# Two-layer cross-attention with image tokens on one core: a written beginning, loads queued behind the stacks, a scaling on ScalarE, and fixed PSUM banks

## The chip, the core and the metric

The kernel runs on one core of a Trainium2 chip. The engines have these names in the profile: PE is TensorE (matrix products; PEld is its weight load), DVE is VectorE, ACT is ScalarE, POOL is GpSimd, SP is SyncE, which issues most DMAs. The metric is the device time of one execution in microseconds (us). Times below are medians of executions without the profiler; every row of a profile comes from one profiled execution of its own.

## The reference

Two cross-attention layers run one after the other. `x` is 16 sequences of 256 queries with 320 channels (20 heads of 16), `ctx` is 16 contexts of 256 tokens with 512 channels. A context is cut into text tokens and image tokens.

```python
# layer 0: text = ctx[:, :77], ip = ctx[:, 77:]
q, k_text, v_text = x @ Wq, text @ Wk, text @ Wv
text_out = softmax(q_h @ k_h.T * scale) @ v_h                    # per head
scores = q_h @ ip_k_h.T * scale                                  # per head
text_probs = softmax(q @ k_text.T * scale)                       # over all channels at once
sem = (text_probs @ text) @ ip.T * scale                         # "semantic" scores
ip_probs = softmax(scores + 0.5 * sem[:, None]) * mask[:, None]  # mask: one number per query
out = (text_out + ip_probs @ ip_v_h) @ Wout + bout + x
# layer 1: text = ctx[:, :-4], ip = ctx[:, -4:]; sem is a cosine, per head, of probs_t @ text with ip;
# otherwise the same form
```

All of it is float32.

## The kernel before, in words

**Numbers in two halves.** A float32 matrix is cut into a rounded high half and a low half (`halves`: a cast on ACT, line 150, and a subtraction on DVE or POOL, line 153). A product is then three products, high x high, high x low and low x high (`prod`, line 238; `prod_m`, line 248, for the queries' and keys' columns, which come in three column blocks m = 0, 1, 2 of 128, 128 and 64 channels). `split` (lines 583 to 585) does the same for the queries' input x (tile `xq`, halves `hq`).

**Slots.** The main loop has 80 slots for layer 0 and 80 for layer 1: slot k is image k // 5 and head group k % 5 (4 heads of 20). A slot of layer 0 consists of

- `score0` for slot k+2, in two halves t = 0, 1 of the queries: four products (line 728) into the tile S, which is two banks of PSUM, and two reduces to maxima on DVE (lines 729, 730);
- `maxima0` for slot k+1: the maxima are turned (line 736, an X tile), copied to `mt`, and written by four small DMAs into the query stack `qs` (line 740); these DMAs are issued by ACT;
- `turned0` for slot k: scores again, keys on partitions (line 752, two T tiles), the exponential on ACT (line 755) into the tiles P in SBUF, and a multiplication by the semantic factor `rs` on POOL (line 758);
- `attend0` for slot k-1: 12 products with the values (line 785) into the PSUM tile P, then `settle0` (lines 796 to 805): a transpose and a normalization on DVE, of which `tmp` (line 802) is the last to read that bank;
- `stacks0` for slot k+4: the slot's keys, queries and semantic rows are brought into the stacks `ks` and `qs` by DMAs of SP. Keys (`kd`) and queries (`qd`) come out of DRAM, where the kernel wrote them after computing them.

**Side work.** What the images need besides is done in pieces between the parts of a slot. A list of tasks gives each piece a due time in slots (`task`, `fill`, `shifted`; `RAMP` compresses times around slot 0): `keys0` (the keys of a pair of images; it starts with the load of a pair's contexts, `context`, tiles `rawc`, halves `cta` and `ctb`), `queries0` (the load of x, `split`, `project` on lines 595 and 598, and a write `qd`), `tokens0` (token products, tile M), `values0_` (values into `vr`, line 401 for the copy), `semantic0` and `close0` (output projection, bias, residual). `semantic0` makes the semantic factor of an image: scores q @ k_text for both halves t (line 651) in an X tile each, copied and summed into `sp` (lines 653, 654), a softmax over the 77 text tokens (maximum, exponential on ACT with its sum, then a reciprocal on line 665 and a multiplication on line 666, both on DVE), a transpose (line 670) whose halves are `tph`, and a product with the tokens.

**Order.** Before the main loop `begin()` runs, in which the order of all engines is the written one: loads of the first contexts and weights (`all_halves`), first keys (`keys_first`), first queries, values and stacks, up to the first slots. In the main loop only PE keeps the written order; SP, ACT, DVE and POOL are ordered by a planner, which issues a load as early as its buffer allows. `queued` ties an instruction behind the last instruction that `anchor` marked on the same engine, without a wait.

**PSUM.** One pool holds 8 banks. A T tile (2 buffers), a P tile (1) or an X tile (3; all side work and the maxima) takes whichever of banks 2 to 7 is free at that point of the plan; the two-bank tile S has banks 0 and 1.

Of the kernel before, what the change touches and what calls it, by code (L numbers as in the profile page):

```python
# [17 lines left out]
S = 256  # L18
# [31 lines left out]
def xattn2(  # L50
# [31 lines left out]
    def dma(out, in_):  # L82
        nc.sync.dma_start(*(f(ap) if ap.dtype == FR else ap for ap in (out, in_)))  # L83
# [43 lines left out]
    nc.scalar.copy(ident_r, ident)  # L127
    tmask = const_tile([128, 7], "tmask")
    dma(tmask, tmask_d)
# [46 lines left out]
    def in_turn(parts, wait, tag="raw", eng=nc.vector):  # L176

        ahead, parts, tags = [], list(parts), tag.split()
        for i in range(len(parts) + 1):
# [6 lines left out]
            for j in new:  # L186
# [4 lines left out]
                dma(raw, src)  # L191
# [27 lines left out]

    def all_halves(jobs, rings):  # L220

        waiting = []
        for src, hi, lo, tag in jobs:
            while sum(w[3] == tag for w in waiting) == rings[tag]:
                halves(*waiting.pop(0)[:3])
            raw = buf(tag, [128, 512], bufs=rings[tag])
            raw = raw[:, : src.shape[1]] if len(src.shape) == 2 else raw.rearrange("p (k n) -> p k n", k=src.shape[1])
            dma(raw, src)
            waiting.append((hi, lo, raw, tag))
        for w in waiting:  # L230
            halves(*w[:3])
# [30 lines left out]
    def context(b, n, wait=0):  # L262
# [8 lines left out]
        yield from in_turn(parts, wait, "rawc raw" if b == 2 and n == 2 else "rawc", nc.gpsimd if wait and b != 2 else nc.vector)  # L271
        if n == 2:
# [3 lines left out]

    ct = [buf(t, [128, 2, 512], FR, bufs=2, name="ct") for t in ("cta", "cta", "ctb", "ctb")]
    ctx0 = [(cT_d[k * 128 : (k + 1) * 128, : 2 * S], ct[k][:, 0], ct[k][:, 1]) for k in range(4)]
# [6 lines left out]
    RINGS = {"P": SIZES["NP"], "raw": SIZES["RAW"], "rawc": 2}  # L285
    all_halves(
        [job for k in range(4) for job in (
            (*ctx0[k], ("rawc", "raw")[k // 2]), (rows(wk0_d, k), *rounded(wkt[:, k]), "P"))],
        RINGS,
    )  # L290
    x0 = buf("xq", [128, 3, S])
    dma(x0, xT_d[0].rearrange("(k p) t -> p k t", p=128))
    all_halves(
# [28 lines left out]
    for v in vr:  # L322
        nc.gpsimd.memset(v, 0.0)
        for t in range(2):
            nc.vector.tensor_scalar_add(
                vcols(v, V0W)[:, t, :, 16], vcols(v, V0W)[:, t, :, 16], tmask[:, t : t + 1]
            )
# [967 lines left out]
```

## Time and profile before

| | before |
|---|---|
| median of 3 runs | 1550.69 us (1549.12 to 1552.69) |
| the profiled execution's own time | 1542.26 us |
| its span | 1540.4 us |
| granted clock of TensorE, mean | 0.978 |
| PE busy | 1441.0 us (94%) |
| DVE busy | 1207.8 us (78%) |
| POOL busy | 1203.6 us (78%) |
| PEld busy | 1162.6 us (75%) |
| ACT busy | 872.8 us (57%) |

The span runs from the first to the last instruction of the profiled execution; its own time has 1.86 us more for what lies around it, and the median of the runs without profiler is 8.43 us above that. Rows of the timeline give start, length, engine and line, operation, tiles written and read, and how many instructions are merged into the row; a bracket at the end gives the idle time before it and what ended it. Rows of waits give who waited, for whom, and then total us, number of waits and the longest. A granted clock of 1.00 is TensorE's full rate.

### The profile page before, as it was taken

The numbers are of one execution on the slowest core, as the hardware profiler recorded it, in microseconds if no ns is written. First come the engines' busy times: TensorE is split into PE (matmuls) and PEld (weight loads), VectorE is DVE, ScalarE is ACT, GpSimd is POOL, SyncE is SP. The second block draws the span as 40 slices with busy tenths as digits, with TensorE's granted clock in tenths as the row PEclk, the third lists the DMA queues.
The fourth block names the chain that finished last, engine by engine and source line by source line (L and its number), as shares of the span: only waits on it lengthen the run. The fifth ranks groups of instructions, "written<-read, shape, count | busy, mean of one in ns | idle before, by whom it ended". The sixth has DMA issues, their size and how long they took to land.

```text
span 1540.4 us, 36105 instructions
## 1 busy us (share of the span) xinstructions
PE 1441.0 (94%) x12726; PEld 1162.6 (75%) x12726; DVE 1207.8 (78%) x2659; ACT 872.8 (57%) x1941; POOL 1203.6 (78%) x1274
## 2 busy tenths in 40 slices
PE   6789999999999989788999999999999999999996
PEld 5678888878787878567777777777777777777764
DVE  6458888777777788867778888888887887788885
ACT  5345555555564545546665666566656666666561
POOL 4258797979797978878587788877987798779785
PEclk9889999999999999989999999999999999999997
DMA  6756777676766666765444344444444344434311
GB/s 208 204 179 175 218 192 215 189 218 188 217 192 201 190 202 172 207 199 153 117 123 117 115 137 110 117 130 120 117 119 136 108 121 124 132 106 113 100 32 36
DMA packets 228815, 233.04 MB, mean 151 GB/s; under 512 B 38410, under 2 KB 198508, under 8 KB 228620
## 3 DMA queue, kind: packets, MB, share of 16 engines
q1 hardware_dynamic: 226428, 229.44, 52.5%
q8 instruction: 102, 1.67, 0.5%
q10 hardware_dynamic: 2208, 1.30, 0.3%
q14 instruction: 77, 0.63, 0.1%
HBM read 118.04 MB, written 77.10 MB: 127 GB/s over the span
## 4 chain that ended last, share of the span: by engine, by line
PE 57%; POOL 12%; DVE 11%; DMA 7%; issue 4%; ACT 3%; SPq 2%; ACTq 1%; DVEq 0%; POOLq 0%
PE X L238 12%; PE X L923 11%; POOL wt L914 5%; PE P L785 5%; PE X L595 5%; PE S L728 4%; PE P L935 3%; PE T L752 3%; PE P L945 3%; PE T L875 2%; PE S L881 2%; POOL P L758 2%; DMA qs<-qd 2%; SPq L83 2%; DVE wt L924 2%
## 5 line engine op out<-in xcount | busy, mean ns | idle before, releaser
L758 POOL TENSOR_TENSOR P<-P,rs 128x512 f32<-128x512 f32 x320 | 413.9, 1316 | 121.0 <-ACT P L755 120.5
L914 POOL TENSOR_TENSOR wt<-P,ctb 128x512 f32<-128x512 f32 x320 | 410.4, 1306 | 86.8 <-ACT ctb L913 85.8
L923 PE MATMUL X<-ctb,gm 128*128 128x512 f32 x1120 | 305.9, 402 | 6.4 <-DVE wt L924 6.3
L755 ACT ACTIVATE P<-T 128x512 f32<-128x512 f32 x320 | 176.3, 594 | 172.7 <-PE T L752 104.4
L924 DVE TENSOR_TENSOR wt<-X,wt 128x512 f32<-128x512 f32 x320 | 216.6, 681 | 46.9 <-PE X L923 41.2
L923 PEld LDWEIGHTS X<-ctb,gm 128*128 128x128 f32 x1120 | 195.7, 189 | 39.8 <-DVE wt L924 9.2
L895 ACT ACTIVATE P<-T 128x512 f32<-128x512 f32 x320 | 173.3, 594 | 76.5 <-PE T L875 74.2
L913 ACT ACTIVATE ctb<-P 128x512 fp32r<-128x512 f32 x320 | 187.0, 627 | 44.1 <-PE X L923 33.1
L883 DVE TENSOR_REDUCE mn<-S 128x4 fp32r<-128x1008 f32 x160 | 191.2, 1195 | 0.0
L730 DVE TENSOR_REDUCE mn<-S 128x4 fp32r<-128x716 f32 x160 | 142.3, 889 | 0.0
L785 PE MATMUL P<-P,vr 128*32 128x256 f32 x1920 | 127.7, 397 | 3.6 <-DVE mx L665 1.2
L728 PE MATMUL S<-ks,qs 125*128 125x256 f32 x640 | 117.5, 307 | 7.5 <-DMA qs<-tph 4.1
L728 PEld LDWEIGHTS S<-ks,qs 125*128 125x128 f32 x640 | 89.0, 196 | 43.1 <-issue 36.2
L752 PE MATMUL T<-qs,ks 127*128 127x256 f32 x640 | 108.4, 290 | 11.9 <-DVE tmp L802 6.4
L1011 POOL TENSOR_TENSOR r<-u,rs 128x40 f32<-128x40 f32 (+2 forms) x17 | 108.7, 6395 | 3.9 <-DVE u L1008 3.8
L752 PEld LDWEIGHTS T<-qs,ks 127*128 127x128 f32 x640 | 90.9, 194 | 14.9 <-DVE tmp L802 6.9
L729 DVE TENSOR_REDUCE mn<-S 128x4 fp32r<-128x308 f32 x160 | 74.2, 464 | 32.4 <-PE S L728 31.6
L796 DVE STREAM_TRANSPOSE nt<-P 128x512 f32<-128x512 f32 x80 | 56.9, 711 | 48.6 <-PE P L785 48.1
L785 PEld LDWEIGHTS P<-P,vr 128*32 128x32 f32 x1920 | 57.4, 112 | 45.6 <-issue 7.0
L595 PE MATMUL X<-hq,wE 128*128 128x256 f32 x512 | 79.2, 294 | 10.6 <-ACT hq L583 5.0
L935 PE MATMUL P<-P,v1t 128*32 128x256 f32 x1280 | 86.4, 388 | 0.2 <-DVE wt L924 0.2
L945 PE MATMUL P<-wt,zone 128*32 128x256 f32 x1280 | 85.1, 379 | 0.3 <-DVE wt L924 0.3
(235 smaller groups left out, 3004.9 us busy)
## 6 DMA issues: line engine op xcount, KB each, us to landing
qd<-q SPq DMA_DIRECT2D x96, 256.0 KB
qs<-tph SPq DMA_DIRECT2D x64, 308.0 KB
rawc<-in_cT_dram SPq DMA_DIRECT2D x60, 256.0 KB
qs<-qd SPq DMA_DIRECT2D x80, 192.0 KB
ks<-kd SPq DMA_DIRECT2D x80, 192.0 KB
ks<-kd SPq DMA_DIRECT2D x160, 96.0 KB
qs<-qd SPq DMA_DIRECT2D x160, 96.0 KB
kd<-kst SPq DMA_DIRECT2D x57, 256.0 KB
```

The lines of the kernel that those rows point to most:

```text
L238: last = mm(out, lhs(a, k), rhs(b, k), start=i == 0, stop=i == len(terms) - 1)
L728: mm(sp[:, h], Q[: XROW + T0, h, t * 128 : (t + 1) * 128], K[: XROW + T0, h], start=True, stop=True)
L752: mm(st[p][:, j], K[:KS0, 2 * p + j, t * 128 : (t + 1) * 128], Q[:KS0, 2 * p + j], start=True, stop=True)
L755: exp = anchor(nc.scalar.activation(pt, st[p], AF.Exp, scale=SCALE))
L758: anchor(nc.gpsimd.tensor_mul(pt, pt, rs[:, t : t + 1].to_broadcast([128, 2, S])))
L785: mm(pv[32 * s : 32 * s + 32, o : o + S], v[:, vt, h : h + 32], P[k, s // 2][:, t, s % 2], start=vt < 2, stop=vt != 1,)
L883: anchor(nc.vector.tensor_reduce(maxes[k + 2][:, t], sp[:, :, :T1], axis=AX.X, op=ALU.max))
L895: anchor(nc.scalar.activation(P[k, u][:, t], st[u], AF.Exp, scale=SCALE))
L913: nc.scalar.activation(R[k, u][:, t], P[k, u][:, t], AF.Copy, scale=0.5)
L914: anchor(nc.gpsimd.tensor_sub(W[k, u][:, t], P[k, u][:, t], f(R[k, u][:, t])))
L923: mm(yp, gm[:, gb], R[k, u][:, kt], start=i == 0, stop=i == len(blocks[n]) - 1)
L924: nc.vector.tensor_mul(W[k, u][:, n], yp, W[k, u][:, n])
```

## The change

Four edits:

- `begin()` is written anew. The loads of the first contexts and weights are issued in an order written there (`first`, `land`, `cast`), `keys_first` makes the text keys of all three column blocks context tile by context tile, the query weights come ahead of the image-token weights, the first stack is issued ahead of the second image's query writes, and the second image's values come later. `constants`, `marks` and `fields` hold what was memsets and small loads: the memset of `qs` and most of that of `vr` go. `turns` gives some X tiles of the beginning a bank of T or P.
- In `context` the loads of both images of a pair (from the third pair on), and in `queries0` those of x for the odd images from image 3 on (`late`), are `queued` behind the key stack's DMA, which is now an anchor on SP. The due time of the odd x load goes from -4.4 to -5.4.
- In `semantic0` the multiplication on line 666 becomes a copy with a scale on ACT.
- In PSUM layer 0 (the profile's first layer) gets fixed tiles: S has its two banks (`whole`), T two of its own and P one (`kept`, taken in turn by `own`); X tiles have the other three. Layer 1 takes its tiles from the pool as before. (The code names the layers 0 and 1.)

```diff
...
+    turns = []
+
     def bank(tag="X"):
-        return ps.tile([128, 512], F32, tag=tag, name=tag, bufs=BANKS[tag])
-
-    def scores():
-
-        return ps.tile([128, 1024], F32, tag="S", name="S", bufs=1).rearrange("p (h t) -> p h t", h=4)
+        turn = turns.pop(0) if turns and tag == "X" else "X"
+        return own(turn) if turn != "X" else ps.tile([128, 512], F32, tag=tag, name=tag, bufs=BANKS[tag])
+
+    whole = ps.tile([128, 1024], F32, tag="S0", name="S", bufs=1)
+    kept = {t: [0] + [ps.tile([128, 512], F32, tag=f"{t}{i}", name=t, bufs=1) for i in range(BANKS[t])] for t in "TP"}
+
+    def own(tag):
+
+        n, *ring = kept[tag]
+        kept[tag][0] += 1
+        return ring[n % len(ring)]
+
+    def scores(kept=False):
+
+        s = whole if kept else ps.tile([128, 1024], F32, tag="S", name="S", bufs=1)
+        return s.rearrange("p (h t) -> p h t", h=4)
...
-                dma(raw, src)
+                (queued if later else lambda inst: inst)(dma(raw, src))
...
-        yield from in_turn(parts, wait, "rawc raw" if b == 2 and n == 2 else "rawc", nc.gpsimd if wait and b != 2 else nc.vector)
+        yield from in_turn(parts, wait, "rawc raw" if b == 2 and n == 2 else "rawc", nc.gpsimd if wait and b != 2 else nc.vector, n == 2 and b > 2)
...
+    def constants():
+
+        nc.vector.memset(zone, 0.0)
+        nc.vector.memset(zone[:, 21:22], 1.0)
+        for i in range(SIZES["NR"]):
+            nc.gpsimd.memset(f(ks[i]), 0.0)
+        nc.gpsimd.memset(f(buf("q", [128, 2, 3, S], FR))[64:, :, 2], 0.0)
+        for v in vr:
+            nc.gpsimd.memset(v[:, :, H * V0W :], 0.0)
+            nc.gpsimd.memset(vcols(v, V0W)[:, 2, :, 16], 1.0)
+
+    def marks():
+
+        for v in vr:
+            for t in range(2):
+                nc.gpsimd.tensor_copy(vcols(v, V0W)[:, t, :, 16], tmask[:, t : t + 1].to_broadcast([128, H]))
+
+    def fields():
+
+        ind0 = buf("nt", [128, 2, 8, 32], bufs=2, name="ind0").rearrange("p a f c -> p (a f c)")[:2, :S]
+        dma(ind0, ind0_d)
+        ind0r = buf("mt", [8, S], FR, name="ind0r")[:2]
+        nc.scalar.copy(ind0r, ind0)
+        for i in range(SIZES["NR"]):
+            dma(ks[i][XROW + T0 : KS0], ind0r.unsqueeze(1).to_broadcast([2, 4, S]))
...
-        for w, lo, hi, a, z in ((wk0, 0, T0 + 1, 0, T0), (wki0, T0 - 1, S, T0, S)):
+        out = lambda lo, hi: bank()[:, : 2 * (hi - lo)].rearrange("p (b t) -> p b t", b=2)
+        kp = [out(0, T0 + 1) for m in range(3)]
+        for k in range(4):
             for m in range(3):
-                kp = bank()[:, : 2 * (hi - lo)].rearrange("p (b t) -> p b t", b=2)
-                prod_m(kp, w, m, lambda s, k: ct(s, k)[:, :, lo:hi], 4)
-                n = 64 if m == 2 else 128
-                evacuate(kst[m][:, 0, :, a:z], kst[m][:, 1, :, a:z], kp[:, :, a - lo : z - lo], m)
-                if a:
-                    keys_out(kd[0][0], m, kst[m], slice(0, 1))
-                else:
-                    nc.gpsimd.tensor_copy(kt[:n, m, :, :, :T0], f(kst[m][:n, :, :, :T0]))
-                yield
+                terms = ((0, 0), (0, 1), (1, 0))[: 3 if m < 2 else 2]
+                for i, (a, c) in enumerate(terms):
+                    mm(kp[m], wk0(a, k, m), ct(c, k)[:, :, : T0 + 1], start=k + i == 0, stop=k == 3 and i == len(terms) - 1)
+            yield
+        for m in range(3):
+            n = 64 if m == 2 else 128
+            evacuate(kst[m][:, 0, :, :T0], kst[m][:, 1, :, :T0], kp[m][:, :, :T0], m)
+            nc.gpsimd.tensor_copy(kt[:n, m, :, :, :T0], f(kst[m][:n, :, :, :T0]))
+        yield
+        for m in range(3):
+            kp = out(T0 - 1, S)
+            prod_m(kp, wki0, m, lambda s, k: ct(s, k)[:, :, T0 - 1 : S], 4)
+            evacuate(kst[m][:, 0, :, T0:], kst[m][:, 1, :, T0:], kp[:, :, 1:], m)
+            keys_out(kd[0][0], m, kst[m], slice(0, 1))
+            yield
...
-    def load(src, tag):
+    def load(src, tag, late=False):
         x = buf(tag, [128, 3, S])
-        dma(x, src.rearrange("(k p) t -> p k t", p=128))
+        order = queued if late else lambda inst: inst
+        order(dma(x, src.rearrange("(k p) t -> p k t", p=128)))
         return x
 
     def queries0(b):
-        x = x0 if b == 0 else load(xT_d[b], "xq")
-        yield
-        xs = split(x, tmask[:, 5:6], nc.gpsimd if b else nc.vector, "hq")
+        x = b and load(xT_d[b], "xq", b > 1 and b % 2)
+        yield
+        xs = split(x, tmask[:, 5:6], nc.gpsimd, "hq") if b else xs0.pop()
         yield
         return (yield from queries(0, xs))
...
             nc.vector.reciprocal(zs, zs)
-            nc.vector.tensor_scalar_mul(tp, tp, zs)
+            nc.scalar.activation(tp, tp, AF.Copy, scale=zs)
...
-                dma(K[0:XROW], stack_rows(kd[0][b // 2][:, :, b % 2], g))
+                anchor(dma(K[0:XROW], stack_rows(kd[0][b // 2][:, :, b % 2], g)))
...
-        sp = scores()
+        sp = scores(True)
...
-        st = [bank("T").rearrange("p (h t) -> p h t", h=2) for p in range(2)]
+        st = [own("T").rearrange("p (h t) -> p h t", h=2) for p in range(2)]
...
-        v, pv = get("v0", b), bank("P")
+        v, pv = get("v0", b), own("P")
...
-        task(("q0", 2 * c + 1), shifted(n, -4.4, -4, -3, -2.8, -2), lambda b=2 * c + 1: queries0(b))
+        task(("q0", 2 * c + 1), shifted(n, -5.4, -4, -3, -2.8, -2), lambda b=2 * c + 1: queries0(b))
...
     def begin():
         parts = lambda *keys: [step(key) for key in keys if key in tasks]
-        k0, q0, s0, m0, q1 = ("k0", 0), ("q0", 0), ("s0", 0), ("m0t", 0), ("q0", 1)
-        parts(k0, k0, k0, q0, q0, q1, q0, q0, q0)
+        k0, q0, s0, m0, m1, q1, v0, v1 = ("k0", 0), ("q0", 0), ("s0", 0), ("m0t", 0), ("m0t", 1), ("q0", 1), ("v0", 0), ("v0", 1)
+        landed = {}
+
+        def land(*names):
+            for n in names:
+                src, hi, lo, tag = first[n]
+                raw = landed[n] = buf(tag, [128, 512], bufs=SIZES["NP"] if tag == "P" else 2)[:, : src.shape[1]]
+                dma(raw, src)
+
+        def cast(*names):
+            for n in names:
+                halves(*first[n][1:3], landed[n])
+
+        named = lambda a: [(a, k) for k in range(4)]
+        for k in range(4):
+            land(("c", k), ("k", k))
+        dma(x0, xT_d[0].rearrange("(k p) t -> p k t", p=128))
+        dma(tmask, tmask_d)
+        constants()
+        for k in range(4):
+            turns.extend(["X"] * (3 if k == 0 else 0))
+            cast(("c", k), ("k", k))
+            parts(k0)
+            if k < 3:
+                land(("q", k))
+        nc.scalar.copy(ident_r, ident)
+        land(*named("i"))
+        xs0.append(split(x0, tmask[:, 5:6], nc.vector, "hq"))
+        for k in range(3):
+            cast(("q", k))
+        nc.vector.tensor_scalar_mul(wqt[:, 2, CH : 2 * CH], f(wqt[:, 2, CH : 2 * CH]), tmask[:, 3:4])
+        land(("v", 0), ("v", 1), ("v", 2))
+        fields()
+        marks()
+        turns.extend(["T", "T", "P", "X", "X", "X", "T"])
+        get(*m0)
+        parts(k0)
+        parts(q0, q0, q0, q0)
+        stacks0(0, "M")
+        parts(q0)
         get(*q0)
-        get(*m0)
-        parts(s0, s0, s0, s0, s0)
-        stacks0(0, "M")
+        cast(("i", 0), ("i", 1))
+        get(*m1)
+        parts(s0)
+        cast(("i", 2))
+        parts(s0)
+        cast(("i", 3))
+        parts(s0, s0, s0)
         stacks0(1, "M")
-        parts(k0, k0, k0, s0, q1, q1, q1, q1)
+        parts(q1)
+        turns.extend(["X", "T", "X", "X"])
+        parts(k0)
+        parts(s0)
+        cast(("v", 0), ("v", 1), ("v", 2))
+        land(("v", 3), *named("w"))
+        parts(k0)
+        cast(("v", 3))
+        parts(k0)
+        stacks0(0, "T")
         stacks0(0, "QK")
+        parts(q1)
+        cast(*named("w"))
         get(*s0)
-        stacks0(0, "T")
-        stacks0(1, "QKT")
-        get("v0", 0)
-        v1 = ("v0", 1)
+        parts(v0, q1, q1)
+        stacks0(1, "TQK")
+        parts(v0)
+        score0(0, 0)
+        parts(q1)
+        get(*q1)
+        parts(v0, k0)
+        get(*v0)
         stacks0(2)
-        parts(k0)
-        score0(0, 0)
-        parts(v1)
         score0(0, 1)
-        get("m0t", 1)
         maxima0(0, nc.sync)
-        parts(v1)
+        parts(v1, v1)
         get(*v1)
-        get(*q1)
         score0(1, 0)
         stacks0(3)
         score0(1, 1)
...
```

More of the change, by code (lines that the diff above doesn't have):

```diff
@@ L174, in rows, with in_turn @@
         return w[k * 128 : (k + 1) * 128]
-    def in_turn(parts, wait, tag="raw", eng=nc.vector):
+    def in_turn(parts, wait, tag="raw", eng=nc.vector, later=False):
         ahead, parts, tags = [], list(parts), tag.split()
@@ L218, in weights_by_row @@
         return lambda s, k, m: parts[k][:, columns(s, m)]
[L220 to L231, printed above, removed]
     def prod(out, lhs, rhs, kt):
@@ L284, in xattn2 @@
     wki0 = lambda s, k, m: wkit[k][:, columns(s, m)]
[L285 to L290, printed above, removed]
-    x0 = buf("xq", [128, 3, S])
-    dma(x0, xT_d[0].rearrange("(k p) t -> p k t", p=128))
-    all_halves(
-        [(rows(wq0_d, k), *rounded(wqt[:, k]), ("rawc", "raw")[k // 2]) for k in range(3)]
-        + [(rows(wki0_d, k), *rounded(w), "P") for k, w in enumerate(wkit)],
-        RINGS,
-    )
```

53 lines of the change are left out of this document (18 added, 35 removed).

## The prediction

> **What bounds the kernel now.** I read the table of stretches first, to see which part of the run has room.
>
> ```profile
> 0.00:68.00 68.00, 46.07 (x270) 42.88 (x271) 35.98 (x112) 28.65 (x72) 19.99 (x29) 0.96 0.71 209
> 400.00:540.00 140.00, 134.37 (x1254) 115.14 (x1252) 109.30 (x248) 78.09 (x179) 117.61 (x112) 0.98 0.68 193
> 540.00:680.00 140.00, 120.82 (x1105) 99.33 (x1105) 114.63 (x248) 70.38 (x167) 110.91 (x128) 0.95 0.69 188
> 900.00:1100.00 200.00, 197.24 (x1747) 153.68 (x1740) 164.83 (x354) 124.78 (x268) 163.81 (x178) 1.00 0.43 122
> ```
>
> Columns: busy time of PE, PEld, DVE, ACT, POOL, then granted clock, DMA share, GB/s. The second layer (900 to 1100) has PE busy for 98.6%, and the change leaves the instruction order of all engines as it was there, so I give it nothing. In the first layer PE is busy for 134.4 of 140: its whole reserve is 5.6 us in 140, more (19.2) where the second layer's weights come in. The beginning has 22 us of idle PE in 68. So only PE's gaps can be won, and I take them from the waits of PE (total, times, longest; 120 to 540, the third 540 to 760, the last 120 to 680):
>
> ```profile
> PE X L736 <- ACT P L755: 3.0, 2, 1.5
> PE T L752 <- DMA qs<-mt: 2.1, 4, 0.7
> PE T L752 <- DVE tmp L802: 6.4, 2, 4.1
> PE X L670 <- DVE sp L666: 3.5, 3, 2.6
> ```
>
> **The beginning.** Timeline, in order of time:
>
> ```profile
> 0.74 0.41 SPq L83 DMA_DIRECT2D rawc<-in_cT_dram  x1
> 4.06 0.62 ACT L150 CAST cta<-rawc 128x512 fp32r<-128x512 f32 x1 [2.04 <-DMA rawc<-in_cT_dram]
> 10.05 0.63 DVE L153 TENSOR_TENSOR wA<-P,wA 128x260 fp32r<-128x260 f32 x3
> 10.82 1.49 PE L238 MATMUL X<-cta,wA 128*128 128x156 f32 x6
> 20.04 3.57 PE L595 MATMUL X<-hq,wE 128*128 128x256 f32 x15 [1.13 <-DVE hq L584]
> 20.84 0.48 SPq L83 DMA_DIRECT2D raw<-in_wvi_dram  x1
> 23.40 1.27 PE L598 MATMUL X<-hq,wE 128*128 128x256 f32 x5
> 26.88 1.01 PE L651 MATMUL X<-kb,q 128*128 128x156 f32 x7 [0.53 <-DVE q L260]
> 29.59 0.26 DVE L666 TENSOR_SCALAR sp<-sp,mx 128x77 f32<-128x77 f32 x1
> 32.34 0.82 PE L248 MATMUL X<-ctb,wB 128*128 128x360 f32 x4
> 34.72 0.52 DVE L260 TENSOR_TENSOR ho<-X,both 64x358 fp32r<-64x358 f32 x1
> 35.69 1.28 SPq L83 DMA_DIRECT2D kd<-ho  x2
> 36.65 2.04 PE L595 MATMUL X<-hq,wE 128*128 128x256 f32 x15 [0.97 <-POOL hq L584]
> 39.18 3.21 SPq L83 DMA_DIRECT2D qd<-q  x5
> 40.47 1.04 PE L238 MATMUL X<-wC,ctb 128*128 128x320 f32 x6
> 43.72 0.95 SPq L83 DMA_DIRECT2D qs<-tph  x1
> 49.11 1.19 PE L728 MATMUL S<-ks,qs 125*128 125x256 f32 x4 [4.07 <-DMA qs<-tph]
> 62.34 0.64 PE L752 MATMUL T<-qs,ks 127*128 127x256 f32 x4
> ```
>
> The first scores (49.11) wait for the first stack's transfer, and on SP that stack stands behind the five writes of the second image's queries (39.18). The written order lets PE do the first key products of all three column blocks as each context tile arrives, brings the query weights ahead of the image-token weights, and issues the stack ahead of the second image's queries. Step by step:
> - Text keys: the last halves are out at 10.68 as now (the eight loads are issued first in both); the last 8 products at 1.49/6 = 0.25 end at 12.7.
> - Token products: 12 of the size of the semantic ones, at 1.01/7 = 0.144, to 14.4. First queries: 21 at 3.57/15 = 0.24, to 19.4, against 24.67 now.
> - Semantic scores ended 3.2 after the queries, and their softmax 2.0 later (29.85): 24.6. The written order puts the halving of weights between; two tiles at 0.63 on DVE make it 25.9.
> - Image-token keys: the first block hides under the softmax; two blocks, 20 products at 0.82/4 = 0.205, make 4.1, and the transposes 0.4: 30.4, against 33.16. Their evacuation took 2.1 (to 35.24), their two writes 1.28: 33.8.
> - The stack reads these keys back from DRAM, so a write and a read lie on the path. The first load of all was used 3.3 after its issue, the stack's 5.4 after it in traffic; two such make 6.6 to 10.8. I take 8.7, as traffic is neither of the two: first scores at 42.5, 6.6 earlier.
> - To the first T there were 13.2. PE now has there four value blocks, 48 products at 1.04/6 = 0.173, 8.3; the second image's last query block, 5 at 0.136, 0.7; 12 semantic products at 1.01/7, 1.7; 20 score products at 0.64/4, 3.2; the reduce of the second scores ahead of the maxima, about 1: 14.9. First T at 57.4, **4.9 earlier**.
>
> What is late next is again the stack's transfer: PE is through its list at 30.4 + 0.5 + 2.1 + 2.2 + 2.1 (sums, a value block, 16 query products, a value block) = 37.3 and idles some 5 us, as it idles 4.07 now. Bounds: at least the five query writes (3.21) leave the first stack's way while four value weights, 0.48 each, come ahead of it: 1.3; at most write and read at 6.6 and a shorter tail: 9. The memsets that vanish from POOL had no one waiting, and cost nothing either way.
>
> **Scaling on ScalarE.** A list by tile gives all 30 later executions (min/median/max ns):
>
> ```profile
> L653 ACT COPY sp<-X x30: 223/228/255, 60.2 to 628.3; 128x77 f32<-128x77 f32 x30
> L666 DVE TENSOR_SCALAR sp<-sp,mx x30: 327/892/1274, 64.3 to 635.2; 128x77 f32<-128x77 f32 x30
> ```
>
> DVE is given back 0.89 twice per image; ACT takes on some 0.23 twice (same shape; its scaled form isn't in the trace: 0.19 to 0.4 by its neighbours). PE's 3.5 of waits for it go but for ACT's own share: **-3.0** (0 to -3.5). The added wait: ACT's two copies stand at the head of its queue until DVE's reciprocal; behind them are the exponentials, and POOL and PE behind those.
>
> **Loads behind the stacks.** Timeline, two slices of the steady part (image pair 1, and 4):
>
> ```profile
> 151.66 0.90 SPq L83 DMA_DIRECT2D rawc<-in_cT_dram  x2
> 154.81 0.38 SPq L83 DMA_DIRECT2D xq<-in_xT_dram  x1
> 194.23 0.55 SPq L83 DMA_DIRECT2D ks<-kd  x1
> 200.94 0.84 ACT L583 CAST hq<-xq 128x768 fp32r<-128x768 f32 x1
> 208.88 1.15 ACT L150 CAST cta<-rawc 128x512 fp32r<-128x512 f32 x2
> 463.23 2.40 ACTq L740 DMA_DIRECT2D qs<-mt  x2
> 465.74 1.09 ACT L755 ACTIVATE P<-T 128x512 f32<-128x512 f32 x2 [3.82 <-DMA qs<-qd]
> ```
>
> Two context loads and one x load are issued at 151.66 and 154.81, some 50 us before their casts (208.88, 200.94), in the busiest stretch of SP. At the same point of pair 4 the small transfers that ACT issues take 2.40 for two, and the exponentials behind them come 3.82 late. In the changed queue these three loads stand 33 to 37 places later, the x load behind the stack at 194.23, the context loads behind the next one. Gain: the 3.0 and 2.1 of PE's waits, **-5.1**. Cover: x has about 6 us from its new issue to its cast, context 8, against 3.3 to 5.4 for a transfer; if the cover fails, ACT stands at the cast. Bounds: -7 to +3 (0.5 at each of six later x loads).
>
> **Banks.** Today an X, T or P tile takes whichever of banks 2 to 7 is free; then, in the first layer, T has two of its own, P one, X three, the scores two. T can no longer get P's bank: the 6.4 go. But X can no longer borrow. One place where that bites:
>
> ```profile
> 149.46 1.14 PE L238 MATMUL X<-cta,wB 128*128 128x360 f32 x6
> 151.83 0.22 DVE L654 TENSOR_TENSOR sp<-sp,X 128x77 f32<-128x77 f32 x1
> ```
>
> With three banks this key product (149.46) follows the semantic scores that DVE reads until 152.05: 2.6 of new wait. In the later pairs DVE comes earlier, so I count two: +5.2. Sum **-1.2** (-6.4 to +10).
>
> **The clock.** A gap costs twice:
>
> ```profile
> 61.80 0.71 PE L728 MATMUL S<-ks,qs 125*128 125x256 f32 x4
> 64.93 0.30 PE L670 MATMUL X<-ident,sp 128*77 128x128 f32 x1 [1.95 <-DVE mx L665]
> 66.21 1.20 PE L728 MATMUL S<-ks,qs 125*128 125x256 f32 x4
> ```
>
> The same four products take 0.71 before a gap of 1.95 and 1.20 after it. In the stretches above the granted clock is 0.98 and 0.95: 2.8 and 7.0 us lost. Half of these 9.8 should go with their gaps, and the two new waits bring some 3 back: **-2** (-9.8 to +6). The Trainium skill (TensorE: Matmul & The Clock Gate, "Part 1: The HAM clock gate") has the clock halved only after an idle window of about 3.4 us; by that the new waits of 2.6 cost no clock and the sum would be 3 lower. The gap of 1.95 speaks against it.
>
> **Sum.** 4.9 + 3.0 + 5.1 + 1.2 + 2 = 16.2 against the profiled execution's 1542.26: 1526.1. The median without profile stands 8.43 higher (1550.69), which I keep: 1534.5, so 1534.
>
> **Rivals.** (1) The beginning wins only its lower bound, 1.3, since the keys' round trip and the queue set it, and new bank waits eat the 1.2: 1534 + 3.6 + 1.2, say 1539. For it: 4.07 of waiting for a transfer now. Against it: the queue really is shorter. (2) ACT's copies hold up the exponentials. DVE's reciprocal can stand behind a pair of reduces on DVE; at 1 us for each of 16 images the gain is gone: 1550, no change. Against it: ACT is busy for only 78.09 of 140. (3) Slower: X with three banks. Each missed bank costs 2.6 and, by the clock rows, as much half-rate time again, some 6. There are 8 pairs; without the two counted waits the sum is 21.4, so it decides from the fourth hit on (3.6 x 6 = 21.6), and six hits give 1550.69 - 21.4 + 36 = 1565. For it: DVE's two-input work is slow beside POOL in every pair. Against it: pairs 4 and 5 have DVE there in time. That the edits do nothing can't be: order and banks are changed in the program as built.
>
> **Chances.** Forecast 0.60, rival 1 0.22, both faster; rival 2 0.07; rival 3 0.11. A difference of 0.2% (3.1 us) is what a measurement here can tell from none. Faster 0.82, same 0.07, slower 0.11. Range: down by most of the better bounds of beginning, clock and banks (15 of 17), 1519; up over rival 1 to the edge of no change, 1549.
>
> **What would show it.** First S product at about 42 and first T at about 57; no wait of T for L802; no wait of L670 for DVE; no ACT gap of over 3 us before exponentials at the pairs' ends; the second layer as long as before. Wrong if the first T comes after 61, if casts of x or context wait for their loads, or if X products wait for DVE reads more than twice.

## The result, and the profile after

| | before | changed |
|---|---|---|
| first measurement, median | 1551.69 us (1549.12 to 1552.90, 4 runs) | 1523.91 us (1520.36 to 1525.92, 4 runs) |
| ratio | | 0.9825 (0.9802 to 0.9847) |
| measured again later, ratio | | 0.9822 (0.9792 to 0.9852) |
| profiled execution, own time | 1542.26 us | 1523.84 us |
| PE busy | 1441.0 us | 1436.5 us |

The forecast was 1534 (1519 to 1549). The time lies in the range, but the gain between the medians is 27.8 us where 16.7 were forecast. Between the two profiled executions it is 18.4 us where the sum said 16.2. So two questions follow: where 18.4 us went, and why the medians differ by 9 us more.

The table of stretches after the change, in the columns used before (busy time of PE, PEld, DVE, ACT, POOL, then granted clock, DMA share, GB/s):

```profile
0.00:68.00 68.00, 50.21 (x291) 45.55 (x291) 37.59 (x104) 33.38 (x85) 18.03 (x39) 0.91 0.77 228
400.00:540.00 140.00, 134.73 (x1269) 115.59 (x1268) 106.01 (x252) 80.39 (x191) 120.63 (x115) 1.00 0.71 204
540.00:680.00 140.00, 120.39 (x1082) 99.32 (x1081) 109.98 (x236) 73.10 (x171) 109.67 (x129) 0.94 0.68 189
900.00:1100.00 200.00, 197.76 (x1759) 153.91 (x1758) 164.99 (x355) 125.59 (x271) 164.56 (x179) 1.00 0.44 122
```

The beginning holds 21 more products in the same 68 us. From 400 to 540 the clock is full and 15 more products fit in. The stretch with the second layer's weights (540 to 680) is not better filled (120.4 us of PE after 120.8, with other products in it, as the run is ahead by then), and the second layer is as it was.

The beginning, from the timeline of PE alone (start, length, line, tiles, shapes, count, idle time before it and its releaser):

```profile
9.08 3.70 PE L390 MATMUL X<-ctb,wA 128*128 128x156 f32 x16
...
14.50 1.42 PE L598 MATMUL T<-hq,wE 128*128 128x256 f32 x8
...
16.70 0.75 PE L601 MATMUL X<-hq,wE 128*128 128x256 f32 x5
...
24.49 0.67 PE L674 MATMUL T<-ident,sp 128*77 128x128 f32 x2 [1.11 <-ACT sp L670]
...
27.64 0.82 PE L246 MATMUL X<-ctb,wB 128*128 128x360 f32 x4
...
32.20 1.43 PE L236 MATMUL X<-wC,ctb 128*128 128x320 f32 x3 [1.94 <-ACT wC L161]
34.37 0.58 PE L598 MATMUL X<-hq,wE 128*128 128x256 f32 x1 [0.75 <-ACT hq L279]
36.02 3.37 PE L598 MATMUL X<-hq,wE 128*128 128x256 f32 x15 [1.07 <-POOL hq L280]
...
40.99 0.68 PE L732 MATMUL S<-ks,qs 125*128 125x256 f32 x4
...
56.22 0.64 PE L756 MATMUL T<-qs,ks 127*128 127x256 f32 x4
```

The first scores come at 40.99 (49.11 before) and no longer wait for the stack's transfer. The first T comes at 56.22 (62.34 before), 6.1 us earlier.

Three rows of PE's waits (120 to 540, 120 to 540, 524 to 744) answer to those shown of before:

```profile
PE X L236 <- DVE sp L658: 2.6, 3, 1.5
PE T L756 <- DMA qs<-mt: 1.5, 3, 0.8
PE X L674 <- ACT sp L670: 4.9, 2, 3.7
```

T no longer waits for P's bank (line 802 before) and the maxima's products no longer wait for the exponentials. New are the X products that wait for the semantic scores' read, as was foreseen. The wait of the transposes is still there. It used to end on VectorE's scaling and now ends on ScalarE's. And the wait for P's bank has not vanished whole: with one bank of its own, P's products wait for line 806, the former 802, at the change of layers (2.0 in two, 524 to 744; 0.8 in two before, 540 to 760).

Three points in the order of T products divide the run the same way in every kernel: the start of slot 10, the start of slot 50, and the second layer's first T. "Before, again" is a second profiled execution of the same unchanged kernel, and "changed, again" is one of the changed kernel; both come from the experiments.

| us | before | before, again | changed | changed, again |
|---|---|---|---|---|
| start to slot 10 | 158.4 | 160.9 | 152.4 | 151.6 |
| slots 10 to 50 | 308.8 | 312.9 | 303.1 | 301.8 |
| slot 50 to second layer | 251.5 | 252.9 | 247.8 | 248.2 |
| second layer, first T to that of its last slot | 781.4 | 782.3 | 780.9 | 779.9 |
| last T to the end | 40.3 | 39.9 | 37.9 | 38.8 |

Against the first profile the gain is 6.0 in the first ten slots, 5.7 in the next forty, 3.7 at the change of layers, 0.5 in the second layer and 2.4 at the very end. The last one is the clock: the final 15 projection products took 3.57 us before and 2.00 after, with nearly the same waits ahead of them, at a granted clock of 0.50 and 0.89 in that stretch. It is not steady: between the two second profiles the end differs by 1.1.

### The profile page after: what moved, and what is told of

It reads as the page before. It is cut to its first block, busy times and chain, and to the rows that moved or that the text cites. A ratio compares the mean times of both kernels' runs of the same rounds, so it can differ in the third digit from the quotient of the medians.

```text
span 1522.1 us, 36012 instructions
## 1 busy us (share of the span) xinstructions
PE 1436.5 (94%) x12726; PEld 1158.2 (76%) x12726; DVE 1180.3 (78%) x2618; ACT 882.0 (58%) x1973; POOL 1195.4 (79%) x1279
## 4 chain that ended last, share of the span: by engine, by line
PE 61%; DVE 11%; POOL 8%; DMA 8%; issue 4%; ACT 4%; SPq 2%; ACTq 1%; DVEq 0%; POOLq 0%
PE X L236 13%; PE X L927 11%; PE P L789 6%; PE X L598 5%; POOL wt L918 5%; PE S L732 5%; PE T L756 4%; PE P L939 3%; PE P L949 3%; PE T L879 2%; PE S L885 2%; DVE wt L928 2%; SPq L83 2%; PE X L246 2%; DVE ho L281 2%
```

## The experiments

The times of a group of kernels were taken on one chip against shared runs of the kernel before. The ratio to it, with its interval, is the measure, and the profile is the explanation. A gain in us is the distance of the ratio from 1, times the median of before in that group.

**One edit alone: the written beginning.** The changed kernel with the other three edits taken back (the context loads and the due time too).

```diff
...
-        return ring[n % len(ring)]
+        return ps.tile([128, 512], F32, tag=tag, name=tag, bufs=BANKS[tag])
...
-        x = b and load(xT_d[b], "xq", b > 1 and b % 2)
+        x = b and load(xT_d[b], "xq")
...
-            nc.scalar.activation(tp, tp, AF.Copy, scale=zs)
+            nc.vector.tensor_scalar_mul(tp, tp, zs)
...
```

> The kernel before with the written beginning alone; loads, scaling and banks as before (no bank turns that are fixed: a T or P tile of the beginning is any free bank). Theory A (the four edits add up, each with the waits it was forecast to remove): first T near 56 as in the changed kernel (62.3 before), and 4 to 6 us faster, ratio 0.996 to 0.9975. Rival B (the 6 us are lost again, since DVE and ACT set the first ten slots): first T near 56 but the slot after ten at its old time (158.4 on the profile), ratio 0.999 to 1.0.

Measured: 1540.18 us against 1548.76, ratio 0.9947 (0.993 to 0.9964), some 8 us, more than theory A's 4 to 6, though the interval reaches the 6. First T at 56.1, slot 10 at 151.2 (158.4 and 160.9 in the two profiles of before). Rival B is out: the head start isn't lost in the first ten slots. The two waits that the loads were to remove still stand in this kernel (slots 10 to 50: T for the maxima's transfer 3.7 us in six, the maxima's products for the exponentials 3.3 in two).

**One edit alone: the loads behind the key stack.**

```diff
...
-                dma(raw, src)
+                (queued if later else lambda inst: inst)(dma(raw, src))
...
-        dma(x, src.rearrange("(k p) t -> p k t", p=128))
+        order(dma(x, src.rearrange("(k p) t -> p k t", p=128)))
...
-                dma(K[0:XROW], ...)
+                anchor(dma(K[0:XROW], ...))
...
-        task(("q0", 2 * c + 1), shifted(n, -4.4, -4, -3, -2.8, -2), ...)
+        task(("q0", 2 * c + 1), shifted(n, -5.4, -4, -3, -2.8, -2), ...)
```

> The kernel before with the context and odd x loads behind the key stack's DMA, and nothing else. Theory A: the waits of the maxima's products for the exponentials (3.0 in two) and of T for the maxima's transfer (2.1 in four) go, 5 us faster, ratio 0.9967. Rival C (the 3.0 are a wait for a bank that an exponential still reads, and so belong to the banks; loads move nothing on PE's path): at most 2 us, ratio 0.9985 to 1.001, and the two waits of 1.5 stay.

Measured: 1543.83 us, ratio 0.998 (0.9957 to 1.0004): about 3 us, not clear of nothing. The two waits of theory A did go. In slots 10 to 50 the second profile of before has them as

```profile
PE X L736 <- ACT P L755: 1.7, 1, 1.7
PE T L752 <- DMA qs<-mt: 1.2, 1, 1.2
```

and here PE waits neither for the exponentials nor with T for the maxima's transfer. But these rows stand there:

```profile
PE X L737 <- DVE mn L731: 2.1, 3, 0.9
PE P L786 <- DVE mx L666: 1.7, 3, 0.6
PE X L671 <- DVE sp L667: 1.4, 3, 0.5
PE X L598 <- ACT mt L739: 1.1, 1, 1.1
PE X L737 <- DMA qs<-tph: 1.0, 1, 1.0
```

The first four are in that profile of before too (2.1, 1.2, 0.9 and 1.0), so some 2 us of the five rows are new. Rival C's mechanism (the two waits stay) is wrong. The gain lies between its 2 us and theory A's 5, and the interval holds both. Four of these five rows are gone when the banks are fixed too (the pair, below).

Two larger waits lie outside these slots, and the kernel before has neither. The scores wait for VectorE's maxima at 140 us, and at the change of layers an X product that has got P's bank waits for line 803, the former 802, which reads that bank (the windows are 120 to 540 and 468.3 to 723.8):

```profile
PE S L729 <- DVE mn L731: 4.2, 1, 4.2
PE X L598 <- DVE tmp L803: 6.2, 1, 6.2
```

VectorE's maxima are late at 140 us because a subtraction ahead of them took 5.91 us. In the two profiles of the kernel before it took 1.8 at most.

```profile
132.37 5.91 DVE L584 TENSOR_TENSOR ho<-hT,ho 128x512 fp32r<-128x512 f32 x1 [1.36 <-ACT ho L583]
```

The loads alone thus take away waits in slots 10 to 50 and bring some 10 us of others; the stretch from slot 50 to the second layer is 255.5 here, against 251.5 and 252.9.

**One edit alone: the scaling on ScalarE.**

```diff
-            nc.vector.tensor_scalar_mul(tp, tp, zs)
+            nc.scalar.activation(tp, tp, AF.Copy, scale=zs)
```

> The kernel before with the scaling of the semantic softmax on ScalarE, and nothing else. Theory A: 3.0 us faster (the waits of the transposes for the scaling), ratio 0.998. Rival D (0.9 us on DVE twice per image also set the reduces behind it, for which the maxima's products wait 5.3 us, and the reciprocal for which P waits 1.2): 6 to 9 us faster, ratio 0.994 to 0.996.

Measured: 1543.89 us, ratio 0.9971 (0.9954 to 0.9987), 4.5 us. The interval holds theory A's 3.0 (ratio 0.998) and excludes the upper part of rival D's.

**One edit alone: the fixed banks.**

```diff
-        sp = scores()
+        sp = scores(True)
-        st = [bank("T")... for p in range(2)]
+        st = [own("T")... for p in range(2)]
-        v, pv = get("v0", b), bank("P")
+        v, pv = get("v0", b), own("P")
```

> The kernel before with layer 1's scores, T and P tiles in fixed banks, and nothing else. Theory A: the 6.4 us of T waiting for P's bank go, two X products wait 2.6 for the semantic scores' reads: about 1 us faster, ratio 0.9985 to 1.0. Rival C: the waits of the maxima's products for the exponentials (3.0) go too and X waits less than was forecast: 6 to 12 us faster, ratio 0.992 to 0.996.

("Layer 1" is the first layer here, the code's layer 0.) Measured: 1547.42 us, ratio 0.9982 (0.9961 to 1.0003), which theory A's 0.9985 fits and rival C's 0.992 to 0.996 does not. Its waits in slots 10 to 50:

```profile
PE T L762 <- DMA qs<-mt: 4.1, 6, 1.1
PE X L605 <- ACT mt L748: 3.2, 4, 0.8
PE X L248 <- DVE sp L664: 2.5, 1, 2.5
```

T now waits six times for the transfer of the maxima, 4.1 us (1.7 and 1.2 in these slots of the two profiles of before). Four of the six, at 239.6, 315.8, 316.8 and 397.2, come 3 to 7 us after context and x loads were issued (from 234.0, 310.2 and 390.5 on). One X product waits 2.5 for the semantic scores' read, the price that was foreseen. T's waits for P's bank, 6.4 us at the change of layers before, are gone there.

The four gains alone add to 8.2 + 3.1 + 4.5 + 2.8 = 18.6 us. The whole change gives 27 to 28. The intervals are wide, so the sums alone do not settle whether the edits add up. The next four kernels take one edit away from the whole, to see which of them are worth more in company.

**All but the beginning.**

```diff
     def begin():
...
-        parts(k0)
-        parts(q0, q0, q0, q0)
-        stacks0(0, "M")
...
+        parts(k0, k0, k0, q0, q0, q1, q0, q0, q0)
+        get(*q0)
+        get(*m0)
+        parts(s0, s0, s0, s0, s0)
+        stacks0(0, "M")
+        stacks0(1, "M")
+        parts(k0, k0, k0, s0, q1, q1, q1, q1)
+        stacks0(0, "QK")
...
```

> The changed kernel with the beginning as before: loads, scaling and banks together. Theory A (edits add up; alone they gave ratios of 0.998, 0.9971 and 0.9982 against before): 10 us faster than before, ratio 0.993 to 0.994. Theory E (each wait that is left costs more than itself, by the clock and by late transfers, so edits are worth more together than alone): 14 to 19 us faster, ratio 0.988 to 0.991.

Measured: 1529.96 us against 1544.75, ratio 0.9901 (0.9871 to 0.9931). That is theory E: three edits that give 10.4 us one by one give 15.3 together, though the interval just reaches theory A's 0.993.

**All but the loads.**

```diff
-        yield from in_turn(parts, wait, ..., nc.gpsimd if wait and b != 2 else nc.vector, n == 2 and b > 2)
+        yield from in_turn(parts, wait, ..., nc.gpsimd if wait and b != 2 else nc.vector)
...
-        x = b and load(xT_d[b], "xq", b > 1 and b % 2)
+        x = b and load(xT_d[b], "xq")
...
-        task(("q0", 2 * c + 1), shifted(n, -5.4, -4, -3, -2.8, -2), ...)
+        task(("q0", 2 * c + 1), shifted(n, -4.4, -4, -3, -2.8, -2), ...)
```

> The changed kernel with the context and odd x loads as early as the planner puts them, as before. Theory A: some 3 us slower than the changed kernel (ratio against before 0.984 to 0.985). Theory E: 5 to 8 us slower than the changed kernel, ratio against before 0.986 to 0.988, and PE waits again for the maxima's transfers or the exponentials at the pairs' ends.

Measured: 1533.08 us, ratio 0.9922 (0.9898 to 0.9945). Against the whole change's 0.9822 (measured below, on another chip) the loads are worth 1.0%, some 15 us, where they gave 3 alone, even more than theory E's 5 to 8. The profile shows 11.6 of them in slots 10 to 50: 6.1 of PE's idle time and 5.5 of its busy time, which is the clock (rows below). The idle time is for the most part one row, 1.3 in two in the changed kernel:

```profile
PE T L756 <- DMA qs<-mt: 6.5, 7, 1.5
```

**All but the scaling.**

```diff
-            nc.scalar.activation(tp, tp, AF.Copy, scale=zs)
+            nc.vector.tensor_scalar_mul(tp, tp, zs)
```

> The changed kernel with the scaling of the semantic softmax on VectorE again. Theory A: 4.5 us slower than the changed kernel (ratio against before about 0.9855). Theory E: 7 to 12 us slower, ratio 0.987 to 0.990: with three banks the X products also wait for the semantic scores that VectorE reads late, and the scaling makes it later.

Measured: 1520.30 us, ratio 0.985 (0.9817 to 0.9884). Its interval takes in theory A's 0.9855 and the whole change's 0.9822, so this run alone tells little except that theory E's 7 to 12 us are unlikely. It was repeated beside the changed kernel, and is told below.

**All but the banks.**

```diff
-        return ring[n % len(ring)]
+        return ps.tile([128, 512], F32, tag=tag, name=tag, bufs=BANKS[tag])
...
-        s = whole if kept else ps.tile([128, 1024], F32, tag="S", name="S", bufs=1)
+        s = ps.tile([128, 1024], F32, tag="S", name="S", bufs=1)
```

> The changed kernel with T, P and score tiles from the pool again, in the beginning too. Theory A: 3 us slower than the changed kernel (ratio against before about 0.9845). Theory E: 6 to 10 us slower, ratio 0.9865 to 0.989, with waits of T for P's bank and of the maxima's products for the exponentials. Rival F (three X banks cost about what the T banks save once everything else is early): no slower, ratio 0.981 to 0.9835.

Measured: 1528.98 us, ratio 0.9911 (0.9877 to 0.9944): the banks are worth 0.9% in company, some 14 us, and 2.8 alone. That is theory E's direction, beyond its 6 to 10; rival F is out. Of the two waits that theory E named, T's for P's bank is there once (3.0, between slot 50 and 540 us), the one for the exponentials is not. In slots 10 to 50 one X product waits 2.8 us until ScalarE has read the maxima, a wait that the changed kernel has in its small form of 0.8 alone:

```profile
PE X L592 <- ACT mt L736: 3.2, 4, 0.8
PE X L595 <- ACT mt L736: 2.8, 1, 2.8
PE T L750 <- DMA qs<-mt: 1.0, 1, 1.0
```

**The pair, loads and banks, on the kernel before.** Both diffs above together.

> The kernel before with the late loads and the fixed banks, without the written beginning and the scaling. Theory A (the edits add): the two ratios 0.998 and 0.9982 multiply to 0.996. Theory E (each of the two takes away one cause of the same late exponentials, so that either cause alone keeps the wait): ratio 0.990 to 0.993, and the maxima's products no longer wait for the exponentials.

Measured: 1537.88 us against 1546.32, ratio 0.9924 (0.9894 to 0.9954) or 11.8 us (8.4 between the medians). Theory A's 0.996 lies outside the interval, and theory E's range holds the ratio. But 0.996 is a product of two measured ratios, and their own intervals reach into that of the pair. The surer sign that the two are worth more together is the kernels without one of them: the intervals of their ratios (0.9898 to 0.9945 and 0.9877 to 0.9944) lie clear of the whole change's (0.9792 to 0.9852), while each alone is not clear of nothing. All that is left of PE's waits in slots 10 to 50:

```profile
PE X L605 <- ACT mt L749: 3.2, 4, 0.8
PE X L747 <- DVE mn L741: 2.2, 4, 0.6
PE X L248 <- DVE sp L665: 0.9, 1, 0.9
```

The same forty slots, one row of the table of stretches for each kernel. PE does the same 2801 to 2803 recorded products in each, so that a difference of its busy time is the clock. First the unchanged kernel's second profile:

```profile
160.90:473.80 312.90, 299.37 (x2802) 257.01 (x2801) 248.47 (x561) 172.11 (x401) 263.69 (x253) 0.99 0.70 202
```

The loads alone:

```profile
160.40:468.30 307.90, 296.30 (x2803) 255.34 (x2802) 250.63 (x561) 172.46 (x400) 263.98 (x253) 1.00 0.70 205
```

The banks alone:

```profile
157.70:475.70 318.00, 305.14 (x2801) 260.86 (x2801) 247.41 (x562) 172.97 (x404) 264.27 (x253) 0.97 0.68 201
```

Loads and banks:

```profile
163.60:467.90 304.30, 296.71 (x2803) 254.97 (x2802) 244.66 (x561) 172.76 (x400) 263.92 (x253) 1.00 0.71 207
```

All but the loads:

```profile
151.80:466.50 314.70, 301.49 (x2803) 257.32 (x2801) 232.28 (x544) 176.06 (x417) 263.01 (x252) 0.98 0.68 199
```

All but the banks:

```profile
153.50:462.60 309.10, 298.33 (x2803) 256.76 (x2802) 234.48 (x545) 176.76 (x417) 263.35 (x253) 0.99 0.70 204
```

The changed kernel:

```profile
152.40:455.50 303.10, 296.00 (x2803) 255.14 (x2802) 231.34 (x545) 176.77 (x417) 262.79 (x252) 1.00 0.72 208
```

Read the first number less the second, PE's idle time: 13.5 before, 11.6 with the loads, 12.9 with the banks, 7.6 with both, 13.2 without the loads, 10.8 without the banks, 7.1 with all. The other profiles agree: 12.9 in the first of before, 16.3 with the beginning alone and 14.0 with the scaling alone; 5.9 in all but the beginning and in the changed kernel again, 7.0 in the latter with the scaling on VectorE, 6.9 in the same kernel's earlier profile. So every kernel with both edits has at most 7.6, and every other at least 10.8. With fixed banks alone T waits for the maxima's transfer when the context loads have just been issued; with late loads alone the transfer is in time, and waits of the kind that the shared banks had remain. Either cause by itself keeps most of the idle time.

PE's busy time is 296 to 297 with both, and up to 305 where the clock fell to 0.97. It is not tied to the pair alone: the loads alone have 296 too, and so has the first profile of before. Nor is each row a typical execution: the profiles of the banks alone and of all but the banks are 4 and 8 us longer than their kernels' medians, that of the pair 6 shorter.

The other half of the story is the change of layers. From slot 50 to the second layer's first T the pair takes 244.5, the loads alone 255.5, the banks alone 254.6, the two profiles of before 251.5 and 252.9. In the pair no X product waits for P's bank any more, and T's 6.4 are gone too. The wait of the scores at some 140 us is in the pair as well, with the long subtraction (4.1 and 5.88). All but the beginning, which is the pair with the scaling on ScalarE, has 1.4 and 1.7 in their place, so the pair alone shows less than the two edits give in company.

**The changed kernel again, and with the scaling on VectorE, side by side.** The edit is that of "all but the scaling".

> The changed kernel as it is, beside the next kernel on the same chip. The first measurement gave a ratio of 0.9825 against before (0.9802 to 0.9847). Expected again: 0.981 to 0.985, whichever theory holds.

> The changed kernel with the scaling of the semantic softmax on VectorE, beside the changed kernel on the same chip. Theory G (once T has its own banks, the next image's factor is no longer on PE's path, and on ScalarE the scaling stands between casts and exponentials that are): 0 to 4 us faster than the changed kernel. Theory A: 3 to 4.5 us slower, as the edit alone gave 4.5.

Measured: ratios to before 0.9822 (0.9792 to 0.9852) and 0.9817 (0.9786 to 0.9849), medians 1521.62 and 1521.36. No worth of the scaling's place is seen in company, which is theory G's lower end. Five runs of each leave some 6 us either way, so theory A's 3 to 4.5 us are not excluded by the times. The trace speaks against their cause: the transposes wait as long with VectorE as with ScalarE (524 to 744, the kernel with VectorE's scaling):

```profile
PE X L674 <- DVE sp L670: 4.6, 2, 2.8
```

No kernel here beats the changed one by more than can be measured; without the scaling edit no difference is seen.

**The kernel before, profiled again.** No edit.

> The kernel before, unchanged, for a second profile and as the scale of the other three. Theory H (its first profile fell on a quick execution, at 1542 where its runs have medians of 1545 to 1552): ratio 0.998 to 1.002, a profiled time of 1544 to 1554, and the excess over the first profile lies in the first layer (first slots and the pairs of images up to 680 us), none in the second.

Measured: ratio 1.0002 (0.9981 to 1.0023), profiled time 1550.76 us, 8.5 more than the first profile's. The profile's line of busy times:

```profile
PE 1446.9 (93%) x12726; PEld 1166.2 (75%) x12726; DVE 1211.1 (78%) x2659; ACT 873.5 (56%) x1941; POOL 1203.2 (78%) x1274
```

The same 12726 products take 5.9 us longer than in the first profile (1441.0): of the 8.5 us, 5.9 are the clock. Nearly as theory H said, the excess lies in the first layer: 2.5, 4.1 and 1.4 in the first three rows of the table above, with 0.9 in the second layer. Of 69 runs of this kernel in the three groups, seven were as quick as 1542.26. The second profile is no typical execution either, 3.6 us above the median of its kernel's twelve runs.

## Why the prediction was right, and where its steps were off

**The beginning: right, one term mis-sized and one reading wrong.** 4.9 us were forecast, the first T came 6.1 earlier, and the edit alone gave 8. The text keys end at 12.78, forecast 12.7. The mis-sized term is the first queries: 21 products at 0.24 each, from a row that followed a wait, made 5.0; they took 2.95 (14.50 to 17.45), at the full clock. The transposes behind the softmax start at 24.49 instead of 25.9 and the image-token keys end at 28.46 instead of 30.4, which is those 2 us. From there on "what is late next is again the stack's transfer" was wrong: nothing waits for it. PE's own list lasts to 40.99. Put at 6.9 us, it took 12.5: 3.8 are waits for the values' weights and for the second image's queries' input, which the list did not have, and the 16 query products took nearly 4 where 2.2 were put. The keys' round trip, put at 8.7, was not what PE waited for. It took at most 6.4, from the end of the last write's issue at 34.59 to the scores, less than the lower bound of 6.6. So the 42.5 was close by luck: one term too long, and a list that was too short. The tail of 14.9 measured 15.2.

**Loads and banks: the waits named rightly, the sum too small, and the split wrong.** They were priced apart, 5.1 and 1.2, each by the waits that it removes. Alone they gave 3.1 and 2.8, neither clear of nothing; together 11.8, and taken out of the whole 15 and 14. The failing step was to treat a wait that ends on one releaser as if nothing else would have ended it a little later. The row of T waiting for the maxima's transfer, 1.7 and 1.2 us in slots 10 to 50 before, grew to 4.1 and 6.5 once the banks were fixed without the loads. And with the loads late and the banks shared, an X product waited 6.2 us for P's bank at the change of layers, where the forecast had counted T's waits only.

**X with three banks: right place, half the price.** 5.2 were set against the gain; the changed kernel shows 2.6 in three waits. Rival 3 needed four hits of 6 us; the three that came are 1.5 at most, and the clock from 120 to 540 stayed full. By the letter, one of the signs of being wrong has shown: X products wait for VectorE's reads three times, where two were allowed (once, 1.4, in the second profile). As a sign it was set too tight, for it counted waits and not their length.

**The scaling: the path wrong.** 3.0 were forecast; 4.5 were measured alone and none seen in company. ScalarE's form took 0.36 per execution, within the 0.19 to 0.4 given. What failed is "PE's 3.5 of waits for it go": the same transposes wait 4.9 us for ScalarE. With the scaling alone they wait 11.3 us in five for it, from 60 us to the second layer, where they waited 4.3 in four before. So the 4.5 us that this edit gave did not come from the wait by which it was priced; where they came from stays open. Rival 2's mechanism is near this, ScalarE's copy standing late, but at the change of layers and not in each image.

**The clock: right in sign, not separable in size.** 2 were forecast. Over the whole run the same 12726 products take 4.5 us less than in the first profile of before (1436.5 for 1441.0) and 10.4 less than in the second. Over slots 10 to 50 the busy time is that of the first profile (295.87 and 296.00), and 3.4 less than that of the second (299.37). The last projection gave 1.6. A clock rule was weighed in the prediction, that of the Trainium skill (TensorE: Matmul & The Clock Gate, "Part 1: The HAM clock gate"), by which an idle window of about 3.4 us halves the clock. With fixed banks alone no wait in slots 10 to 50 was longer than 2.5 us, and the granted clock there was 0.97; the measurement decides against reading the rule as a free allowance for shorter gaps. In that kernel the clock fell where T waited twice in one slot: it was 0.66 from 160 to 170, after waits that ended at 158.8 and 159.9, and 0.79 from 320 to 330, after 315.8 and 316.8. After single waits of 0.7 and 1.1 (239.6 and 397.2) the next 10 us had 1.00. In all but the loads it fell after two such pairs (0.83 and 0.66) and not after a third, so this is no rule yet.

**The base of the sum: prices from a quick execution.** Between the two profiled executions the sum was 2.2 us off, which is partly luck, as its terms missed singly. Between the medians it was 11 short. 8.43 was carried over as the distance from profile to median, and the changed kernel's profiled time is its median within 0.1. The second profile of before, 8.5 us longer than the first, has 5.9 more of busy time for the same products and 2.6 more of idle time. So the rows from which the terms were priced came from an execution in which clock and waits cost less than they mostly do.

## What to carry to other kernels

A row of waits names the last of several causes: before pricing an edit by the wait that it ends, ask what would have ended that wait next, and try edits that share a place in pairs, as loads and banks here gave 11.8 us together and 5.9 as the sum of each alone, with wide intervals. A bank of its own for the tile on the path pays only if the data for it are in time, so move bulk loads out of the stretch in which small transfers are waited for. Moving loads moves what stands behind them: look at the whole run for waits that are new, and not only at the slots in which old ones went. One profiled execution can lie near the edge of its kernel's runs: compare its time with theirs before its rows are taken as prices.

## What the runs showed of the hardware that was not expected

Executions of the kernel before spread over 22 us (69 runs in three groups, 1536.65 to 1558.37), those of the changed kernel over 10 (nine runs, 1517.03 to 1527.50). Between the two profiles of before, 5.9 of 8.5 us are the time of the same products. That fewer waits make the time steadier fits this, but nine runs do not show it.

The scaling on VectorE varied by a factor of nearly five, with POOL's work beside it. In the beginning, with POOL idle, it took 264 ns, later 327 to 1274. In the kernel before, by the timeline around the first slot:

```profile
63.46 2.48 POOL L758 TENSOR_TENSOR P<-P,rs 128x512 f32<-128x512 f32 x2 [23.59 <-ACT P L755]
64.27 0.52 DVE L666 TENSOR_SCALAR sp<-sp,mx 128x77 f32<-128x77 f32 x1
64.89 1.12 DVE L666 TENSOR_SCALAR sp<-sp,mx 128x77 f32<-128x77 f32 x1
```

The second one ends at 66.01, with POOL's second multiplication, which ends at 65.94. On ScalarE the same work keeps its time (the changed kernel's list by tile, minimum, median and maximum in ns):

```profile
L670 ACT ACTIVATE sp<-sp,mx x30: 343/361/365, 58.4 to 620.2; 128x77 f32<-128x77 f32 x30
```

The Trainium skill (SBUF — State Buffer, "Who interferes with whom") says that a VectorE tensor_scalar can take a port pair that it shares with GpSimd, with the later of the two blocked until the other is done, while TensorE and ScalarE wait for nobody. The rows agree, 327 to 1274 on the one and 343 to 365 on the other. In the whole change no gain from it is seen, because the scaling was not the last thing that PE's transposes lacked.

The longest case of a VectorE instruction beside POOL's is the subtraction of 5.91 us in the kernel with the loads alone. It starts at 132.37, and POOL goes through five instructions without a gap from 132.32 to 137.74. The same form took 0.67 where it was quickest. In the changed kernel it took 1.69 at most. That POOL held it up fits the times; no run took POOL's work away to show it.
